# A gated unit with one quantized matmul: the order's cost table repriced, late weight ranges on ScalarE, one rounding step fewer for down_w

## The chip, the cores and the metric

The kernel runs on one core of one Trainium2 chip. The metric is the device time of one execution in microseconds (us); lower is better. Five instruction streams run side by side and wait for each other by semaphores: PE (TensorE), DVE (VectorE), ACT (ScalarE), POOL (GpSimd) and SP (SyncE, which issues nearly all DMAs here). Each stream is carried out strictly in its own order: an instruction that waits holds up everything behind it on its engine.

## The reference

```python
def act_quant(x):      # per token
    scale = 127.0 / clip(max(abs(x), axis=-1, keepdims=True), 1e-05)
    return clip(round(x * scale), -128, 127) / scale
def weight_quant(w):   # one scale for the whole matrix
    scale = 1.0 / clip(mean(abs(w)), 1e-05)
    return clip(round(w * scale), -1, 1) / scale

scale = cond @ norm_w.T + 1.0                       # (4, 512)
h = x * (scale[:, None, :] * rsqrt(mean(x*x, -1) + 1e-6))
u = h @ up_w.T                                      # (4, 1024, 4096)
val, gate = split(u, 2, axis=-1)
h = val * gelu(gate)                                # (4, 1024, 2048)
y = act_quant(h) @ weight_quant(down_w).T + x       # (4, 1024, 512)
```

x is (4, 1024, 512) in float32, cond (4, 128), norm_w (512, 128), up_w (4096, 512), down_w (512, 2048).

## The kernel before

There are four batches of 1024 tokens, and the 2048 hidden features are cut into 16 groups of 128 (index j), each with a gate row block and a value row block of up_w. Weights and activations are split into two float16 parts, so a product takes three float16 matmul terms. The first batch uses the plain product (`plain`, L897 in the profile), half by half of the tokens; while it runs, the weights are loaded, ranged, scaled, turned and their sums built and spilled to `s_dram`. Batches 1 to 3 use seven products of sums in place of eight (`product`, L882, driven by `slot`), and the quantized second matmul of the batch before runs in between (`Pair`, L1153, and `down_mm`, L1102).

Names and steps that the change and the prediction touch:

- `w_range(j)` is `w_largest` (L589: largest magnitude of each row of up_w's two blocks of group j, one DVE reduce) and `w_factor` (power of two of it, its reciprocal); `w_scale` multiplies the rows by it. Only a power of two is needed, so that the rows fit float16.
- down_w comes in eight parts, `d_load(n)`. `d_sum(n)` sums magnitudes on ACT (L744), `d_mean` (L753) brings their mean over the partitions by one matmul, `d_round(n)` scales, clips and rounds on DVE (L759, L760), `d_put(n)` writes the -1, 0, 1 as 8-bit floats on ACT (L769).
- The condition: `scT` holds the row scale of each batch with the features along the partitions. `cond_rows` (L551) writes the columns of batches 1 to 3 to `rows_dram`, three DMAs of 512 single floats each. `cond_load_scale(b)` (L556) reads row b back to every partition as `sc`; `cond_bring(b, sc)` (L560) multiplies it on DVE. The tokens of the next batch are then scaled with it (`Tokens.scale`).
- In `plain_half(j, h)` the gate product goes to bank A or B and through Gelu on ACT, the value product goes to bank E, and a DVE step (L925) multiplies them into H. It is this DVE step that frees the E bank; there are two E banks, taken in turn.

Nothing runs in the order of the source. `Plan` records every instruction as a `Step` with a cost from `price()` (alone, beside a busy neighbour, and for a DMA the time that it holds the queue). `order()` makes 40 rounds: `needed` gives each step the latest time at which it may start, `place` puts the steps one after another, most urgent first, into the first free stretch of their engine, and `replay` runs the resulting order in the model, six times with random misses. The best order is emitted, engine by engine. So a change of a price moves instructions on all five engines. In the model a DMA lands 1.2 us (ISSUE) plus its queue time plus 1.5 us (LANDING) after its issue; the queue time is its bytes by 290, 150 or, for runs under 64 bytes, 1.5 KB per us.

Of the kernel before, what the change touches and what calls it, by code (L numbers as in the profile page):

```python
# [22 lines left out]
P = 128  # L23
EXPONENT = 0x7F800000
MAGIC = 1.5 * 2.0**23
# [2 lines left out]


W_UP = 2.0**12  # L30
X_UP = 2.0**8


# [78 lines left out]
class Plan:  # L112
# [68 lines left out]
    def order(self):  # L181

        steps = self.steps
        for s in steps:
            s.after, s.cost = [], (s.alone + s.beside) / 2
        for s in steps:
            for d in s.deps:
                steps[d].after.append(s)
        clock = 0.0
        for s in steps:  # L190
            if s.eng == "PE":
                s.start = clock
                clock += s.cost
        best, chance = None, random.Random(1)
        for n in range(ROUNDS):
            self.needed(clock)
            self.place(0.3 * (n % 4))
            order = sorted(steps, key=lambda s: (s.start, s.n))
            clock = self.replay(order)
            late = sum(self.replay(order, chance) for _ in range(MISSES)) / MISSES  # L200
            if best is None or late < best[0]:
                best = late, order
            self.replay(order)
        self.replay(best[1])
        return best[1]
# [5 lines left out]
            for t in s.after:  # L211
                s.late = min(s.late, t.late - lag(s, t) - s.wait - s.cost)

    def place(self, margin):

        steps = self.steps
        used = {e: Line() for e in ("PE", "ACT", "DVE", "POOL", "SP", "DMA")}
        for s in sorted(steps, key=lambda s: (s.late, s.n)):  # L220
            t = max((steps[d].end + lag(steps[d], s) for d in s.deps), default=0.0)
            if s.eng != "PE":
                t += min(margin, max(0.0, s.late - t) * 0.1)
            if s.wait and s.eng == "SP":
                t = used["DMA"].put(t + ISSUE, s.wait) - ISSUE
            s.start = used[s.eng].put(t - s.before, s.before + s.cost) + s.before
            s.end = s.start + (ISSUE + s.wait + LANDING if s.wait else s.cost)

    def replay(self, order, chance=None):

        steps = self.steps
        free = dict.fromkeys(("PE", "ACT", "DVE", "POOL", "SP", "DMA"), 0.0)
        port = {"DVE": 0.0, "POOL": 0.0}
        for s in order:
            e = s.eng
            t = free[e] + s.before
# [26 lines left out]


HEAD = 150
ROUNDS, MISSES, ISSUE, LANDING, RELOAD = 40, 6, 1.2, 1.5, 6.5


class Line:
# [2 lines left out]
    def __init__(self):  # L272
        self.spans = []

    def put(self, t, cost):
# [7 lines left out]
        v.insert(n, (t, t + cost))  # L283
        return t


# [9 lines left out]
def price(eng, method, writes, reads, args, kwargs):  # L296

    out = writes[0]
    n = _free(out)
    if "dma" in method:  # L300
        nbytes = n * out.shape[0] * mybir.dt.size(out.dtype)
        if "transpose" in method:
            return 0.45 + nbytes / 32768 * 0.16, 0.0, nbytes / 32768 * 0.17
        last = min(v.ap[-1][1] * mybir.dt.size(v.dtype) if v.ap[-1][0] == 1 else 4 for v in (out, reads[0]))
        return 0.45, 0.0, nbytes / (290e3 if last >= 1024 else 1.5e3 if last < 64 else 150e3)
    wide = max([n] + [_free(v) for v in reads if len(v.shape) > 1])
    psum = any(str(v.space).endswith("PSUM") for v in reads)
    if eng == "PE":
        f32 = any(v.dtype == F32 for v in reads)
        return (max(n, 64) * (2 if f32 else 1) / 2.4 + 2.5) / 1e3, 0.0, 0.0  # L310
    if eng == "ACT":
        cost = 0.08 + wide * 0.0009 + (0.05 if method != "copy" else 0) + (0.05 if psum else 0)
        return cost, 0.0, 0.0
    if eng == "POOL":
        if method == "partition_all_reduce":
            return (1.8 if wide > 1 else 0.4), 0.0, 0.0
        if method == "tensor_scalar":
            cost = 0.2 + wide * 0.00092
            return cost, cost * 1.2, 0.0
        cost = 0.75 if wide <= 8 else 0.18 + wide * 0.00195  # L320
        return cost, cost * 1.42, 0.0
    if method == "reciprocal":
        return 0.17 + max(0, wide - 8) * 0.0056, 0.0, 0.0
    if wide <= 32:
        return 0.17, 0.0 if psum else 0.44, 0.0
    if psum or method in ("tensor_reduce", "memset"):
        return 0.1 + wide * 0.00108, 0.0, 0.0
    if method == "tensor_scalar":
        cost = 0.1 + wide * 0.00052
        return cost, cost * 2.2, 0.0  # L330
# [3 lines left out]
    cost = 0.1 + wide * 0.00106  # L334
    return cost, cost * (1.35 if method == "scalar_tensor_tensor" else 1.8), 0.0


class Rings:
# [30 lines left out]
def glu_quant_kernel(  # L369
# [11 lines left out]
    PE, ACT, DVE, POOL, SP = book.engines(nc)  # L381
# [12 lines left out]
    cpool = ctx.enter_context(tc.tile_pool(name="const", bufs=1))  # L394
# [3 lines left out]
    psum = Rings(banks, {"A": 512, "B": 512, "E": 512, "po": 512})  # L398
# [4 lines left out]
    one = cpool.tile([P, 1], F32, name="one")  # L403
    DVE.memset(one, 1.0)
    ones = one.to_broadcast([P, P])

    R = cpool.tile([P, 2, NA * 2048], F32, name="R")  # L410
# [38 lines left out]
        "p (c w f) -> p c w f", c=7, w=2  # L449
    )  # L450
    A21 = R[:, 0, 6144 : 6144 + 768].bitcast(F16).rearrange("p (n w f) -> p n w f", n=3, w=2)

    def s_tile(g):

# [108 lines left out]
    sw = cpool.tile([P, NJ, 2], F32, name="sw")  # L563
# [6 lines left out]
    def wn(j):  # L570
        return H[:, W_SLOT[j % 3]]
# [14 lines left out]
    def w_largest(j, t0=0, t1=2):  # L586
        t = slice(t0, t1)
        am = sm.tile([P, 2], F32, name=f"wam_{j}_{t0}", tag="wam")[:, t]
        DVE.tensor_reduce(am, wn(j)[:, t], AX.X, ALU.max, apply_absolute_value=True)  # L589
        return am  # L590

    def w_factor(j, am, t0=0, t1=2):
        t = slice(t0, t1)
        pow2_floor(am)
        DVE.tensor_scalar(sw[:, j, t], am, 2.0**-100, 1.0 / W_UP, ALU.max, ALU.mult)
# [130 lines left out]
    wsc = cpool.tile([P, 1], F32, name="wsc")  # L726
# [4 lines left out]
    def d_part(n):  # L731
        return R[:, 1, n * HF : (n + 1) * HF]
# [23 lines left out]

    def d_round(n):
        dn = d_part(n)
        DVE.tensor_scalar(dn, dn, wsc, 1.0, ALU.mult, ALU.min)  # L759
        DVE.tensor_scalar(dn, dn, -1.0, MAGIC, ALU.max, ALU.add)  # L760

    tn = []

    def d_put(n):
        _, u, y = d_at(n)
        if y == 0:
            tn.append(wpool.tile([P, HF], BF16, name=f"tn_{n}", tag="v"))
        t8 = tn[-1].bitcast(F8).rearrange("p (f y) -> p f y", y=2)
        ACT.activation(t8[:, :, y], d_part(n), AF.Copy, bias=-MAGIC, saturate=False)  # L769
        if y:  # L770
            SP.dma_start_transpose(wd[:, n // 4, u], tn[-1])

# [505 lines left out]
    am = w_largest(0, 1, 2)  # L1278
# [317 lines left out]
    for b in range(1, B):  # L1596
        dve, act = Filler(), Filler()
        gains(b)
        am = am_tile(b - 1)
# [42 lines left out]
        for j in range(NJ):  # L1642
# [7 lines left out]
            more = D_SUM_US * len(late_sums) + 0.7 * (j + 1 == min(DOWN) and b + 1 < B)  # L1650
# [77 lines left out]
    am = am_tile(b)  # L1728
# [160 lines left out]
```

## Time and profile before

| what | value |
|---|---|
| runs of the kernel before | 742.14, 742.27 and 743.57 us; median 742.27 |
| the profiled execution | 737.92 us, its span 736.1 us |
| granted TensorE clock in it | 0.998 of full speed |
| PE busy | 723.8 us (98% of the span) |
| DVE, ACT, POOL busy | 606.6 (82%), 392.1 (53%), 215.5 us (29%) |
| DMA queue of SP | 114.76 MB, 60.7% of the 16 engines' span |

The profiled execution is 4.35 us quicker than the median of the runs; its span leaves out 1.8 us of its own time. PE is the engine that is nearly always busy, so the time hangs on the few places where PE waits, and on what stands before its first and behind its last matmul.

### The profile page before, as it was taken

What the parts mean: (1) busy time and instruction counts of PE and PEld (TensorE: products, weight loads), DVE (VectorE), ACT (ScalarE), POOL (GpSimd) and SP (SyncE); (2) the same over time, 40 slices, a digit from 0 to 9 for tenths busy, and PEclk for the clock granted to TensorE, in tenths of its full rate; (3) what the DMA queues carried; (4) which work ended last, traced back from release to release, by engine and by line L of the source; (5) the groups of instructions that cost most, each with busy time, mean ns of one, the idle gap of its engine ahead of it and who ended that gap; (6) DMA issues with size and microseconds to landing.
All of it is one profiled execution on the core that took longest, in us unless ns stands there. A gap on an engine that the chain in (4) does not pass through costs nothing.

```text
span 736.1 us, 10201 instructions
## 1 busy us (share of the span) xinstructions
PE 723.8 (98%) x3684; PEld 363.2 (49%) x3684; DVE 606.6 (82%) x833; ACT 392.1 (53%) x635; POOL 215.5 (29%) x213
## 2 busy tenths in 40 slices
PE   6999999999999999999999999999999999999998
PEld 3554444444444445655444445656444444444754
DVE  5976899999888767989878988798768888865997
ACT  4876646676245775535344577743333666333373
POOL 1465887789214000714002300750001000000000
PEclk9999999999999999999999999999999999999999
DMA  8788678999954444695943445697753444443414
GB/s 267 244 175 206 192 203 210 233 250 236 229 162 101 100 102 137 159 206 154 233 135 101 108 101 140 159 208 155 183 141 106 97 100 108 104 101 97 144 38 164
DMA packets 179567, 115.74 MB, mean 157 GB/s; under 512 B 141750, under 2 KB 147767, under 8 KB 179516
## 3 DMA queue, kind: packets, MB, share of 16 engines
q1 hardware_dynamic: 179226, 114.76, 60.7%
q10 hardware_dynamic: 290, 0.33, 0.3%
q8 instruction: 29, 0.48, 0.3%
q14 instruction: 22, 0.18, 0.1%
HBM read 58.93 MB, written 23.09 MB: 111 GB/s over the span
## 4 chain that ended last, share of the span: by engine, by line
PE 88%; DMA 5%; DVE 3%; ACT 3%; issue 1%; POOL 1%; SPq 0%; POOLq 0%; DVEq 0%
PE A L882 33%; PE E L882 17%; PE B L882 8%; PE po L1153 8%; PE E L897 8%; PE B L897 4%; PE A L897 4%; DMA rows_dram<-scT 2%; PE po L1102 2%; PE E L1102 1%; PE A L1102 1%; DMA s_dram<-R 1%; DMA H<-in_x_dram 1%; DMA am<-in_x_dram 1%; ACT R L1218 1%
## 5 line engine op out<-in xcount | busy, mean ns | idle before, releaser
L882 PEld LDWEIGHTS <-SXY 128*128 128x128 f16 x2016 | 197.2, 98 | 229.8 <-issue 2.1
L882 PE MATMUL A<-R,SXY 128*128 128x512 f16 x1152 | 270.5, 379 | 0.3 <-ACT t L960 0.3
L882 PE MATMUL E<-R,SXY 128*128 128x512 f16 x576 | 142.9, 379 | 0.0
L1032 POOL PARTITION_ALL_REDUCE am<-R x8 | 17.3, 2158 | 249.1 <-DVE R L1018 249.1
L1074 DVE TENSOR_TENSOR H<-H,am 128x1024 f32<-128x1024 f32 x64 | 78.7, 1260 | 0.1
L897 PEld LDWEIGHTS <-SXY 128*128 128x128 f16 x462 | 45.1, 98 | 53.5
L882 PE MATMUL B<-R,SXY 128*128 128x512 f16 x288 | 70.8, 379 | 0.0
L1016 DVE TENSOR_REDUCE gm<-H 128x512 f32<-128x1024 f32 x56 | 68.9, 1230 | 0.7
L980 DVE SCALAR_TENSOR_TENSOR H<-A,sg,t 128x512 f32<-128x512 f32 x48 | 35.9, 748 | 36.0 <-PE A L882 35.7
L968 ACT COPY B<-A 128x512 f32<-128x512 f32 x48 | 27.4, 570 | 60.1 <-PE A L882 56.7
L1153 PE MATMUL po<-wd,R 128*128 128x256 fp8e4 (+1 forms) x448 | 59.0, 275 | 0.0
L993 ACT ACTIVATE t<-t,sg 128x512 f32<-128x512 f32 x48 | 34.7, 722 | 39.2 <-DVE t L990 39.1
L1153 PEld LDWEIGHTS <-R 128*128 128x128 bf16 (+1 forms) x480 | 47.0, 98 | 15.9
L960 ACT COPY t<-A 128x512 f32<-128x512 f32 x48 | 28.1, 586 | 48.9 <-PE A L882 48.8
L990 DVE TENSOR_TENSOR t<-E,t 128x512 f32<-128x512 f32 x48 | 33.0, 688 | 24.4 <-PE E L882 24.0
L977 ACT ACTIVATE t<-B,sg 128x512 f32<-128x512 f32 x48 | 33.0, 687 | 34.5 <-PE B L882 34.0
L786 POOL TENSOR_SCALAR ssq<-ssq 128x2 f32<-128x2 f32 x12 | 5.5, 456 | 155.4 <-ACT H L816 114.1
L897 PE MATMUL E<-R,SXY 128*128 128x512 f16 x210 | 49.6, 379 | 0.0
L996 DVE TENSOR_TENSOR v<-A,v 128x512 f32<-128x512 f32 x48 | 33.1, 689 | 19.7 <-PE A L882 18.0
L972 ACT COPY v<-E 128x512 f32<-128x512 f32 x48 | 28.1, 586 | 34.0 <-PE E L882 31.6
L1018 DVE TENSOR_TENSOR R<-R,gm 128x512 f32<-128x512 f32 x56 | 44.4, 792 | 0.8
L897 PEld LDWEIGHTS <-R 128*128 128x128 f16 x282 | 27.5, 98 | 33.6 <-issue 1.3
(232 smaller groups left out, 1082.0 us busy)
## 6 DMA issues: line engine op xcount, KB each, us to landing
SXY<-s_dram SPq DMA_DIRECT2D x66, 256.0 KB, 2.7
SXY<-s_dram SPq DMA_DIRECT2D x18, 384.0 KB, 3.6
H<-in_L_cond_up_w_dram SPq DMA_DIRECT2D x13, 512.0 KB, 4.9
s_dram<-SXY SPq DMA_DIRECT2D x14, 384.0 KB, 4.9
xr<-in_x_dram SPq DMA_DIRECT2D x19, 256.0 KB, 3.3
out_dram<-xr SPq DMA_DIRECT2D x19, 256.0 KB, 3.6
H<-in_x_dram SPq DMA_DIRECT2D x8, 512.0 KB, 5.5
R<-in_L_cond_down_w_dram SPq DMA_DIRECT2D x8, 512.0 KB, 6.5
```

The costliest lines, as they stand in the source:

```text
L882: PE.matmul(o, s[:, w, k, :], tv[:, :, c, l, k, :], start=start and n == 0, stop=stop and n == len(TERMS) - 1, skip_group_check=True,)
L897: PE.matmul(ps, a[k // 2][:, w, k % 2, :], XP[:, l, k, h * TOK : (h + 1) * TOK], start=n == 0, stop=n == len(terms) - 1,)
L977: ACT.activation(cur["t1"], pb, AF.Gelu, scale=gain(g, 1))
L980: DVE.scalar_tensor_tensor(h_half(g - 1, 0), prev["A"], gain(g - 1, 0), prev["t1"], ALU.mult, ALU.mult)
L990: DVE.tensor_tensor(prev["t2"], prev["E"], prev["t2"], ALU.add)
L993: ACT.activation(prev["t2"], prev["t2"], AF.Gelu, scale=gain(g - 1, 1))
L996: DVE.tensor_tensor(cur["v"], cur["A"], cur["v"], ALU.add)
L1016: DVE.tensor_reduce(gm[0], v, AX.X, ALU.max, apply_absolute_value=True)
L1018: return [largest, lambda: DVE.tensor_tensor(m, m, gm[0], ALU.max)]
L1074: DVE.tensor_tensor(v, v, r.to_broadcast([P, 2, TOK]), ALU.mult)
L1102: PE.matmul(po.rearrange("p (y c o) -> p y c o", c=2, o=P), q[:, a, h, j], wd8[:, :, j // n, j % n, :, y0:y1].rearrange("p c o y -> p y c o"),
L1153: PE.matmul(po, w[:, j], m, start=start and j == 0, stop=stop and j == n - 1, skip_group_check=True,)
```

## The change

Four edits, of which the first moves instructions all over the program:

1. The model of the planner. DMAs issued by other queues than SP's are placed and replayed like SP's. `place` takes a second number (`guard`, a stretch kept free ahead of an urgent step), with four settings of both in turn. Random misses are drawn otherwise. Prices of ACT, DVE and POOL steps are changed.
2. For groups 6 and up, `w_largest` is two ACT passes with Abs and a running sum over the row, in place of one DVE reduce; the sum stands in for the largest value, and W_UP for it is twice as large.
3. `d_round` is one DVE step (scale, then add a large constant, which rounds) and no longer clips; `d_put` takes Sign of the value less that constant.
4. A small constant tile is filled at the start (`nmagic`).

```diff
+BY_SUM = 6
+W_UP_SUM = 2.0**13
...
-            self.place(0.3 * (n % 4))
+            self.place(*MARGINS[n % len(MARGINS)])
...
-    def place(self, margin):
+    def place(self, margin, guard):
...
-            if s.wait and s.eng == "SP":
+            if s.wait > 0.1:
                 t = used["DMA"].put(t + ISSUE, s.wait) - ISSUE
-            s.start = used[s.eng].put(t - s.before, s.before + s.cost) + s.before
+            near = 0.0 if s.eng == "PE" or s.late - t > 1.0 else guard
+            s.start = used[s.eng].put(t - s.before, s.before + s.cost, near) + s.before
...
-                cost *= 1.0 if e == "PE" else 0.95 + 0.14 * chance.random()
+                cost *= 1.0 if e == "PE" else 0.96 + 0.12 * chance.random()
+                if s.beside > s.alone:
+                    cost += 0.6 * (s.beside - s.alone) * chance.random()
...
-            if s.wait and e != "SP":
+            if 0.0 < s.wait <= 0.1:
                 s.end = t + ISSUE + s.wait + LANDING
...
+MARGINS = ((0.3, 0.0), (0.3, 0.15), (0.3, 0.3), (0.25, 0.1))
...
-        cost = 0.08 + wide * 0.0009 + (0.05 if method != "copy" else 0) + (0.05 if psum else 0)
+        cost = 0.12 + wide * 0.0008 + (0.05 if psum else 0)
+        if wide == 512 and method != "copy":
+            cost = 0.62 if psum else 0.7
...
     def w_largest(j, t0=0, t1=2):
...
+        if j >= BY_SUM:
+            for n in range(t0, t1):
+                ACT.activation(w_junk, wn(j)[:, n], AF.Abs, accum_out=am[:, n : n + 1])
+            return am
         DVE.tensor_reduce(am, wn(j)[:, t], AX.X, ALU.max, apply_absolute_value=True)
...
     def d_round(n):
         dn = d_part(n)
-        DVE.tensor_scalar(dn, dn, wsc, 1.0, ALU.mult, ALU.min)
-        DVE.tensor_scalar(dn, dn, -1.0, MAGIC, ALU.max, ALU.add)
+        DVE.tensor_scalar(dn, dn, wsc, MAGIC, ALU.mult, ALU.add)
...
-        ACT.activation(t8[:, :, y], d_part(n), AF.Copy, bias=-MAGIC, saturate=False)
+        ACT.activation(t8[:, :, y], d_part(n), AF.Sign, bias=nmagic, saturate=False)
```

What the new prices do to the order is shown at four places. Lines of the changed kernel are 16 to 21 higher than those of the kernel before: its L567, L572, L576, L917, L945, L774 and L1213 are L551, L556, L560, L897, L925, L753 and L1193 there.

The first place is SP's queue in the first 70 us, in the kernel before. `rows_dram<-scT` is `cond_rows`, `sc<-rows_dram` is `cond_load_scale(1)`, `H<-in_L_cond_up_w_dram` a load of up_w, `xn` and `am` loads of tokens of batch 1:

```order
L693 DMA s_dram<-SXY 128x3584
L740 DMA R<-in_L_cond_down_w_dram 128x1024 x2
L808 DMA xn_109<-in_x_dram 128x2x512
L551 DMA rows_dram<-scT 128x4x1 x2
L693 DMA s_dram<-SXY 128x3584
L581 DMA H<-in_L_cond_up_w_dram 128x2x512
L556 DMA sc_112<-rows_dram 128x512
L808 DMA am_114<-in_x_dram 128x2x512
L581 DMA H<-in_L_cond_up_w_dram 128x2x512
L551 DMA rows_dram<-scT 128x4x1
L693 DMA s_dram<-R 128x3584
```

The same place of SP's queue in the changed kernel:

```order
L714 DMA s_dram<-SXY 128x3584
L761 DMA R<-in_L_cond_down_w_dram 128x1024 x2
L714 DMA s_dram<-SXY 128x3584
L597 DMA H<-in_L_cond_up_w_dram 128x2x512
L828 DMA xn_110<-in_x_dram 128x2x512
L597 DMA H<-in_L_cond_up_w_dram 128x2x512
L567 DMA rows_dram<-scT 128x4x1
L828 DMA am_115<-in_x_dram 128x2x512
L572 DMA sc_113<-rows_dram 128x512
L714 DMA s_dram<-R 128x3584
L567 DMA rows_dram<-scT 128x4x1 x2
L714 DMA s_dram<-SXY 128x3584
```

The first row of the condition went from ahead of two loads of up_w to behind them, with the read of it two places after it; the other two rows follow the read. The second of the two loads of up_w ahead of it waits until PE has turned the weights that lie in its place. On PE, these four transposes (L625 before, L646 now) stood behind the fourth matmul of a gate product into bank B; now they stand in the gate product before it, into bank A, behind the four matmuls that follow the transposes of the group's other block.

The second place is DVE at the same time. Here is the kernel before, from the last range of a weight group to the multiplication of the next half (`gm` is a maximum over H for the token ranges):

```order
L598 RECIPROCAL iv_101<-sw 128x2
L604 TENSOR_SCALAR sg_77<-sw,dx 128x2 x2
L925 TENSOR_SCALAR H<-E_98,sg_77,t_1_104 128x512
L560 TENSOR_SCALAR sc_112<-sc_112,ux 128x512
L1016 TENSOR_REDUCE gm_106<-H 128x512
L660 TENSOR_TENSOR R<-po_97,R 128x256
L1018 TENSOR_TENSOR R<-R,gm_106 128x512
L658 TENSOR_TENSOR R<-po_96,R 128x2x256
```

And DVE in the changed kernel:

```order
L619 RECIPROCAL iv_102<-sw 128x2
L625 TENSOR_SCALAR sg_78<-sw,dx 128x2 x2
L576 TENSOR_SCALAR sc_113<-sc_113,ux 128x512
L1036 TENSOR_REDUCE gm_107<-H 128x512
L945 TENSOR_SCALAR H<-E_99,sg_78,t_1_105 128x512
L775 TENSOR_SCALAR wmean<-po_96 128x1
L776 RECIPROCAL wsc<-wmean 128x1
L780 TENSOR_SCALAR R<-R,wsc 128x1024
```

The step that empties the first of the two E banks stood ahead of `cond_bring`; now it stands behind it and behind a reduce.

The third place is PE right there. In the kernel before (E_98 and E_99 are the two E banks, the `po<-ident,H` rows transposes of weights):

```order
L897 LDWEIGHTS R
L897 MATMUL E_99<-R 128x512
L897 LDWEIGHTS R
L897 MATMUL E_99<-R 128x512
L625 MATMUL po_96<-ident,H 128x128 x4
L897 LDWEIGHTS SXY
L897 MATMUL B_87<-R,SXY 128x512
```

In the changed kernel (E_99 is here the first E bank, E_100 the second):

```order
L917 LDWEIGHTS R
L917 MATMUL E_100<-R 128x512
L774 MATMUL po_96<-wpart_112,one 128x1
L917 LDWEIGHTS R
L917 MATMUL E_99<-R 128x512
L917 LDWEIGHTS R
L917 MATMUL E_99<-R 128x512
L917 LDWEIGHTS R
L917 MATMUL E_99<-R 128x512
```

Where the transposes and a gate product followed, there now follow the mean's matmul and four matmuls into the first E bank, taken from later in the stream.

The fourth place is DVE in batch 2, near 490 us, where the second matmul's third pair ends. L865 casts the tokens of the next batch, L1193 takes a bank of the second matmul out. Before:

```order
L1138 TENSOR_TENSOR R<-R 128x1024
L999 TENSOR_SCALAR H<-v_117,sg_77,t_1_124 128x512
L865 TENSOR_TENSOR H<-H 128x4x256
L1193 TENSOR_SCALAR xr_125<-po_95,dq_127,xr_125 128x256
L1193 TENSOR_SCALAR xr_126<-po_95,dq_127,xr_126 128x256
```

In the changed kernel, where L1157, L1158 and L1019 are L1137, L1138 and L999 of the kernel before:

```order
L1157 TENSOR_TENSOR R<-H,R 128x1024
L1158 TENSOR_TENSOR R<-R 128x1024
L1019 TENSOR_SCALAR H<-v_118,sg_78,t_1_125 128x512
L1213 TENSOR_SCALAR xr_126<-po_96,dq_128,xr_126 128x256
L1213 TENSOR_SCALAR xr_127<-po_96,dq_128,xr_127 128x256
```

The cast of the tokens no longer stands between the multiplication and the two steps that empty the bank; it was moved up.

More of the change, by code (lines that the diff above doesn't have):

```diff
@@ L273, in __init__, with put @@
         self.spans = []
-    def put(self, t, cost):
+    def put(self, t, cost, guard=0.0):
         v = self.spans
@@ L282, in put @@
             n += 1
-        v.insert(n, (t, t + cost))
+        free = v[n - 1][1] if n else 0.0
+        v.insert(n, (max(free, t - guard), t + cost))
         return t
@@ L320, in price @@
         cost = 0.75 if wide <= 8 else 0.18 + wide * 0.00195
-        return cost, cost * 1.42, 0.0
+        return cost, cost * (1.2 if wide > 256 else 1.42), 0.0
     if method == "reciprocal":
@@ L326, in price @@
     if psum or method in ("tensor_reduce", "memset"):
-        return 0.1 + wide * 0.00108, 0.0, 0.0
+        return 0.1 + wide * (0.00116 if wide == 512 else 0.00105), 0.0, 0.0
     if method == "tensor_scalar":
-        cost = 0.1 + wide * 0.00052
-        return cost, cost * 2.2, 0.0
+        cost = 0.08 + wide * 0.00051
+        return cost, cost * 1.85, 0.0
     if method == "tensor_tensor" and all(v.dtype in (BF16, F16) for v in reads):
@@ L333, in price @@
         return cost, cost * 1.6, 0.0
-    cost = 0.1 + wide * 0.00106
-    return cost, cost * (1.35 if method == "scalar_tensor_tensor" else 1.8), 0.0
+    cost = 0.1 + wide * 0.00101
+    more = 1.45 if wide > 512 or method == "scalar_tensor_tensor" else 1.8
+    return cost, cost * more, 0.0
 class Rings:
@@ L405, in glu_quant_kernel @@
     ones = one.to_broadcast([P, P])
+    nmagic = cpool.tile([P, 1], F32, name="nmagic")
+    DVE.memset(nmagic, -MAGIC)
     R = cpool.tile([P, 2, NA * 2048], F32, name="R")
@@ L451, in glu_quant_kernel @@
     A21 = R[:, 0, 6144 : 6144 + 768].bitcast(F16).rearrange("p (n w f) -> p n w f", n=3, w=2)
+    w_junk = R[:, 0, 5888:6144].bitcast(BF16)
     def s_tile(g):
@@ L594, in w_factor @@
         pow2_floor(am)
-        DVE.tensor_scalar(sw[:, j, t], am, 2.0**-100, 1.0 / W_UP, ALU.max, ALU.mult)
+        up = W_UP_SUM if j >= BY_SUM else W_UP
+        DVE.tensor_scalar(sw[:, j, t], am, 2.0**-100, 1.0 / up, ALU.max, ALU.mult)
         if j not in iv:
```

## The prediction

> **What bounds the kernel now.** I read the page first, then the windows, then who PE waited for, then the chain of work in order of time.
>
> ```profile
> span 736.1 us, 10201 instructions
> ...
> PE 723.8 (98%) x3684; PEld 363.2 (49%) x3684; DVE 606.6 (82%) x833; ACT 392.1 (53%) x635; POOL 215.5 (29%) x213
> ```
>
> PE is idle for 12.3 us of 736.1 (736.1 - 723.8). The windows say where; the second column of a row is its length, the third PE's busy time in it:
>
> ```profile
> 0.00:20.00 20.00, 13.70 (x55) 7.26 (x55) 11.10 (x56) 9.13 (x20) 2.56 (x8) 0.91 0.75 246
> ...
> 60.00:80.00 20.00, 18.95 (x93) 9.13 (x91) 16.05 (x31) 15.72 (x28) 13.84 (x16) 1.00 0.59 153
> ...
> 220.00:260.00 40.00, 39.71 (x186) 18.12 (x185) 31.38 (x37) 25.21 (x35) 8.82 (x8) 1.00 0.40 95
> ...
> 460.00:500.00 40.00, 39.02 (x252) 24.50 (x251) 35.05 (x44) 22.99 (x47) 25.16 (x24) 1.00 0.75 169
> ...
> 720.00:736.10 16.10, 12.61 (x75) 7.06 (x72) 11.82 (x18) 5.17 (x5) 0.00 (x0) 1.00 0.45 164
> ```
>
> 6.3 us are lost before the first weights and tokens are there, 3.5 us behind the last matmul, and between them only 1.05, 0.29 and 0.98 us (another 0.16 stands in 20 to 40 us). So a better order can win some 2.5 us at the most, and a worse one can lose more: PE has no slack to give a wait back. The waits of PE name the middle two:
>
> ```profile
> PE E L897 <- DVE H L925: 1.0, 1, 1.0
> PE po L1153 <- DVE xr L1193: 1.0, 1, 1.0
> ```
>
> The chain of work between 40 and 80 us shows what stands behind the first:
>
> ```profile
> 41.38 12.25 DMA rows_dram<-scT
> ...
> 54.08 6.37 DMA am<-in_x_dram
> ...
> 64.65 7.88 DMA s_dram<-R
> ...
> 79.19 1.02 PE E L897 x4
> ```
>
> The reader is to see that the small scatter of the condition is the longest piece of this chain: 12.25 us from its issue to its landing, for 2 KB. It cost nothing itself, because nobody needed it soon.
>
> **The change, part by part.** The edits of the work itself come first, by groups of instructions (after the bar: busy time in all, mean ns of one):
>
> ```profile
> L589 DVE TENSOR_REDUCE wam<-H 128x2 f32<-128x1024 f32 (+1 forms) x17 | 19.5, 1147 | 4.2 <-DMA H<-in_L_cond_up_w_dram 4.2
> ...
> L760 DVE TENSOR_SCALAR R<-R 128x1024 f32<-128x1024 f32 x8 | 8.8, 1123 | 0.0
> ...
> L769 ACT ACTIVATE v<-R 128x1024 fp8e4<-128x1024 f32 x8 | 8.4, 1052 | 1.1 <-DVE R L760 0.9
> ...
> L816 ACT ACTIVATE xt<-xn 128x512 f32<-128x512 f32 x12 | 7.5, 626 | 1.6 <-DMA xn<-in_x_dram 1.5 <-DVE nx L865 0.2
> ...
> L816 ACT ACTIVATION_READ_ACCUMULATOR xt<-xn 128x1 f32 x12 | 2.3, 189 | 0.0
> ```
>
> Ten groups (6 to 15) lose a reduce of 1.15 us, so DVE is rid of 11.5 us, and of 8 x 1.12 = 9.0 us with the second rounding step. ACT takes on 20 passes; no such pass with Abs on 512 elements is in the trace, the nearest is the sum of squares, 0.63 us and 0.19 us for reading the sum out: 20 x 0.82 = 16 us. `d_put` with Sign in place of a copy I take at the same 1.05 us. All of it lies between 60 and 190 us, where every window but the quoted one shows PE fully busy, and ACT has room (15.7 of 20 us in that one). I cost this edit at zero for the end; without that cover, 16 us of ACT against 20 us of DVE in one stretch would shift a wait by tenths. The fill of one constant at the start I take at zero too (under 0.1 us on DVE).
>
> The new order is what counts. **The gain** is at 495 us:
>
> ```profile
> 492.76 1.74 DVE L865 TENSOR_TENSOR H<-H 128x1024 f16<-128x1024 f32 x1
> ...
> 493.98 0.38 PE L882 MATMUL A<-R,SXY 128*128 128x512 f16 x1
> ...
> 494.42 0.86 DVE L1193 SCALAR_TENSOR_TENSOR xr<-po,dq,xr 128x256 f32<-128x256 f32 x2
> ...
> 495.34 0.27 PE L1153 MATMUL po<-wd,H 128*128 128x256 fp8e4 x1 [0.98 <-DVE xr L1193]
> ```
>
> PE waits for the pair of steps at 494.42, which stood behind a cast of 1.74 us. The order of the changed kernel has no cast between; the pair comes up to 1.74 us earlier, and the wait goes: 495.34 - 493.98 less one matmul of 0.2 is 1.15 us. I take 1.1 us; next late there are steps that were on time before.
>
> **The loss** is near 67 us. These are the rows of the kernel before:
>
> ```profile
> 41.38 0.97 SPq L551 DMA_DIRECT2D rows_dram<-scT  x2
> ...
> 50.58 1.67 PE L897 MATMUL A<-R 128*128 128x512 f16 x7
> ...
> 53.70 0.33 SPq L556 DMA_DIRECT2D sc<-rows_dram  x1
> ...
> 55.54 0.60 PE L625 MATMUL po<-ident,H 128*128 128x128 f32 x4
> ...
> 56.17 0.37 SPq L581 DMA_DIRECT2D H<-in_L_cond_up_w_dram  x1
> 56.60 0.94 SPq L551 DMA_DIRECT2D rows_dram<-scT  x1
> ...
> 66.75 0.60 PE L625 MATMUL po<-ident,H 128*128 128x128 f32 x4
> 66.87 0.74 DVE L925 SCALAR_TENSOR_TENSOR H<-E,sg,t 128x512 f32<-128x512 f32 x1
> ...
> 67.53 0.47 DVE L560 TENSOR_SCALAR sc<-sc,ux 128x512 f32<-128x512 f32 x1
> ...
> 67.92 1.23 DVE L1016 TENSOR_REDUCE gm<-H 128x512 f32<-128x1024 f32 x1
> ```
>
> Step by step. (a) The first row of the condition was issued at 41.38. Now it follows a load of up_w which waits for the four transposes of 55.54; these come after four of the seven matmuls at 50.58 (each 1.67 less 0.17 of the last one's run-out, by 7: 0.21 us), so at 51.4, and end at 52.0. The load goes at 52.0, the row at 52.4 (0.4 behind, as 56.60 behind 56.17): 11 us later than before. (b) How long it takes and the read of it after it, by the DMA view (us to landing last):
>
> ```profile
> sc<-rows_dram SPq DMA_DIRECT2D x3, 256.0 KB, 4.3
> ...
> rows_dram<-scT SPq DMA_DIRECT2D x3, 2.0 KB, 12.1
> ...
> dq<-am_dram SPq DMA_DIRECT2D x2, 2.0 KB, 2.4
> ```
>
> SP issues the read when the row has landed (53.70 follows 41.38 by 12.3 us), and tokens, spills and two more rows of the condition wait behind it on SP. With the rows' 12.1 and 4.3 us, `sc` is there at 68.8. Two rows of 512 single floats went together at 41.38, behind two parts of down_w and a load of tokens; now it is one, behind one load. That can take off what lay ahead in the queue, so I take 11.0 and 4.2: `sc` at 67.6. (c) On DVE, `cond_bring` (0.47) waits for that, the reduce (1.23) and the multiplication that frees the E bank (0.74) stand behind it, with three hand-overs of 0.05: 2.6 us, so the bank is free at 70.2. (d) PE reaches the four matmuls into this bank where the kernel before stood at 66.75, plus one small matmul for the mean: 66.8. It waits 70.2 - 66.8 = 3.4 us. Before, the multiplication was done at 67.6 without any DMA and the bank was used much later.
>
> From below, the nearest small transfer took 2.4 us; with it nothing waits at all, since the read then lands at 59.1, and the wait is zero from a landing of `sc` at 64.2 downwards. From above, 12.25 for the row and the 6.37 us that the chain shows behind the first read give 71.0 and a wait of 6.8 us. I take 3.4, near the rows of the very same transfer.
>
> [...]
>
> What else moves? The other two rows are issued together behind the read, with a spill of 896 KB behind them. In the chain the spill at 64.65 took 7.88 us with the third row 8 us ahead of it. That chain led to the 1.05 us of wait at 79.19. In the new order the spill from R goes ahead of those rows, the one from SXY behind; I leave the 1.05 as it is, with 1 us on either side. Head and tail keep their order but for single steps, zero with 0.3 on either side.
>
> Sum: 3.4 - 1.1 = +2.3 us. The profiled execution would go from 737.92 to 740.2, its span from 736.1 to 738.4. The runs' median was 742.27; the same difference gives 744.6.
>
> **The rivals.**
>
> *The row lands in time (faster).* Place: `cond_bring` on DVE. The point is `sc` at 64.2, that is 11.8 us for row and read together. For it: the 2.4 us of the other 2 KB transfer, a queue with less ahead, one row in place of two. Against: 12.25 us in the chain, 12.1 in the DMA view. [...] The rival gives -1.1, or -2.2 if the wait at 79.19 goes too, since then the spill no longer stands behind the rows: 740.1 to 741.2.
>
> *Wait and gain cancel.* Row and read take 12 to 14.4 us, the wait is 0.2 to 2.6 us: 741.4 to 743.8.
>
> *The wait is long.* Row and read take 12.25 and 6.37 us as in the chain, or the spill behind the two later rows holds up the loads of up_w behind it as the 7.88 us did: wait 5 to 6.8, with 1 us more at 79: +3.9 to +6.7, 746.2 to 749.
>
> *The edits don't take work off DVE.* The prices move the steps anyway and PE has no DVE wait left of that kind; it changes none of these sums.
>
> **How the numbers follow.** A measurement here tells about 0.2%, 1.5 us. The forecast (wait 2.6 to 5 us, 743.8 to 746.2) has 0.50, the long wait 0.11, cancelling 0.19, in time 0.20, of which 0.13 with the wait at 79.19 gone too (-2.2) and 0.07 without (-1.1). Slower by over 0.2% is the forecast and the long wait, 0.61; within 0.2% cancelling and the smaller part of in time, 0.26; faster 0.13. The range 740.6 to 748.0 takes in the forecast, the cancelling, most of in time and the lower part of the long wait; it leaves out at most 2 in 10.
>
> **What would show it.** In the profile of the changed kernel: `cond_bring` on DVE, near 68 us, waiting for the DMA of `sc`; PE waiting 2 to 5 us for the multiplication into H, in the window 60 to 80, whose PE time falls to 14 to 17 us; the row's issue near 52 and the read's near 63; no wait at L1213 near 495. Wrong would be: `sc` landed before 64, PE waiting somewhere else by more than 1.5 us, or the window 460 to 500 still short of 1 us.

## The result and the profile after

| | before | changed |
|---|---|---|
| runs, us | 737.47 to 743.57, median 741.45 (12 runs) | 743.22 to 748.06, median 746.31 (12 runs) |
| profiled execution, us | 737.92, span 736.1 | 745.51, span 743.7 |
| ratio | | 1.0068, 95% interval 1.0047 to 1.0089 |

The changed kernel is slower: 0.0068 of 741.45 us is 5.0 us (3.5 to 6.6 by the interval). The forecast was +2.3 us. The time lies inside the predicted range, near its upper end, but just above the forecast's own band (743.8 to 746.2) and at the lower edge of the rival "the wait is long". The page of the changed kernel, with the busy time of the engines:

```profile
span 743.7 us, 10243 instructions
PE 725.1 (97%) x3684; PEld 362.7 (49%) x3684; DVE 595.4 (80%) x816; ACT 405.5 (55%) x675; POOL 213.0 (29%) x213
```

DVE has lost 11.2 us of work and ACT has gained 13.4, in the direction that the edits meant. The groups taken off DVE held 20.9 us before (12.1 of ranges, 8.8 of rounding), against 20.5 forecast; not all of it shows, because other steps of DVE took longer in sum. PE was idle for 18.6 us in place of 12.3. Its windows, with the granted clock behind the engines' columns:

```profile
0.00:20.00 20.00, 14.61 (x65) 6.89 (x66) 13.16 (x61) 11.20 (x23) 3.14 (x8) 1.00 0.69 233
...
60.00:80.00 20.00, 14.51 (x62) 7.13 (x61) 7.57 (x13) 7.61 (x15) 6.29 (x9) 0.83 0.82 100
80.00:100.00 20.00, 17.32 (x81) 7.78 (x80) 19.93 (x19) 15.86 (x26) 18.11 (x16) 1.00 0.81 241
...
460.00:500.00 40.00, 40.00 (x248) 24.16 (x247) 32.43 (x42) 19.69 (x39) 20.20 (x23) 1.00 0.75 172
```

460 to 500 us is full now: the wait of 0.98 us there is gone. 60 to 80 us lost 5.5 us of PE's time and 80 to 100 us 2.7. PE there, in order of time:

```profile
64.48 0.28 PE L774 MATMUL po<-wpart,one 128*128 128x1 f32 x2
69.79 1.87 PE L917 MATMUL E<-R 128*128 128x512 f16 x4 [5.03 <-DVE H L945]
71.45 1.70 PE L646 MATMUL po<-ident,H 128*128 128x128 f32 x7
73.62 0.48 PE L646 MATMUL po<-ident,H 128*128 128x128 f32 x1 [0.46 <-ACT R L672]
73.88 3.42 PE L917 MATMUL B<-R,SXY 128*128 128x512 f16 x12
...
86.90 1.02 PE L917 MATMUL E<-R 128*128 128x512 f16 x4 [2.69 <-DVE H L945]
```

There are two waits, 5.03 and 2.69 us. Behind the first PE runs at half speed: four matmuls take 1.87 us, those at 86.90 take 1.02, and the granted clock is 0.83 in 60 to 80 us and 1.00 in 80 to 100. What the queue of SP and the waiting engines did:

```profile
50.27 0.46 SPq L567 DMA_DIRECT2D rows_dram<-scT  x1
...
61.80 0.34 SPq L572 DMA_DIRECT2D sc<-rows_dram  x1
62.24 0.38 SPq L714 DMA_DIRECT2D s_dram<-R  x1
62.67 1.52 SPq L567 DMA_DIRECT2D rows_dram<-scT  x2
64.30 1.68 SPq L714 DMA_DIRECT2D s_dram<-SXY  x1
```

```profile
67.46 0.49 DVE L576 TENSOR_SCALAR sc<-sc,ux 128x512 f32<-128x512 f32 x1 [6.26 <-DMA sc<-rows_dram]
...
69.00 0.74 DVE L945 SCALAR_TENSOR_TENSOR H<-E,sg,t 128x512 f32<-128x512 f32 x1
```

```profile
76.51 0.59 ACT L670 CAST R<-po 128x512 f16<-128x512 f32 x1 [2.94 <-DMA s_dram<-R]
```

```profile
77.12 0.69 DVE L679 TENSOR_TENSOR R<-po,R 128x512 f16<-128x512 f32 x1 [2.57 <-ACT R L670]
```

```profile
64.30 17.26 DMA s_dram<-SXY
```

The reader is to see two chains. One is the forecast's: row, read, `cond_bring`, multiplication, E bank. The other was given only a tolerance: the spill from R, issued at 62.24, is waited for by ACT until 76.51, and DVE waits for ACT until 77.12. From there DVE works without a gap over 0.2 us up to the multiplication of 86.11 to 86.85 that PE's second wait ends with. The spill from SXY takes 17.26 us in the chain of work. Both spills stand beside three rows of the condition.

### The profile page after: what moved, and what is told of

The parts are those of the page before. It is cut to its first block, busy times and chain, and to the rows that moved or that the text cites. A ratio compares the mean times of both kernels' runs of the same rounds, so it can differ in the third digit from the quotient of the medians.

```text
span 743.7 us, 10243 instructions
## 1 busy us (share of the span) xinstructions
PE 725.1 (97%) x3684; PEld 362.7 (49%) x3684; DVE 595.4 (80%) x816; ACT 405.5 (55%) x675; POOL 213.0 (29%) x213
## 4 chain that ended last, share of the span: by engine, by line
PE 91%; DVE 4%; DMA 3%; ACT 1%; issue 1%; SPq 0%; DVEq 0%; ACTq 0%
PE A L902 33%; PE E L902 17%; PE E L917 10%; PE po L1173 8%; PE B L902 8%; PE A L917 6%; PE B L917 5%; DMA s_dram<-SXY 2%; DVE H L1094 2%; DMA H<-in_x_dram 1%; PE A L1122 1%; PE B L1173 0%; PE po L646 0%; DVE am L1063 0%; PE A L960 0%
## 5 line engine op out<-in xcount | busy, mean ns | idle before, releaser
L1052 POOL PARTITION_ALL_REDUCE am<-R x8 | 15.6, 1946 | 285.5 <-DVE R L1038 285.5
L917 PEld LDWEIGHTS <-SXY 128*128 128x128 f16 x462 | 45.4, 98 | 54.5 <-issue 0.8
L917 PE MATMUL E<-R,SXY 128*128 128x512 f16 x210 | 49.7, 379 | 0.0
L917 PE MATMUL E<-R 128*128 128x512 f16 x162 | 39.9, 385 | 7.7 <-DVE H L945 7.7
L917 PEld LDWEIGHTS <-R 128*128 128x128 f16 x282 | 27.7, 99 | 40.2 <-issue 8.6
L1102 ACT ACTIVATE H<-H 128x1024 f32<-128x1024 f32 x38 | 40.0, 1056 | 8.6 <-DVE H L1094 8.6
L1038 DVE TENSOR_TENSOR R<-R,gm 128x512 f32<-128x512 f32 x56 | 42.9, 765 | 0.9
```

The source lines that it names most:

```text
L917: PE.matmul(ps, a[k // 2][:, w, k % 2, :], XP[:, l, k, h * TOK : (h + 1) * TOK], start=n == 0, stop=n == len(terms) - 1,)
L1038: return [largest, lambda: DVE.tensor_tensor(m, m, gm[0], ALU.max)]
L1102: ACT.activation(v, v, AF.Copy, bias=MAGIC)
```

## The experiments

Two theories were put against each other. A: PE waits because the multiplication stands behind `cond_bring`. B: what counts is that spills and loads beside the single floats land late, whatever stands in front on DVE. The moves were written into the finished order, so that nothing else changed; each pair is (step, the step it goes ahead of):

```diff
-        return best[1]
+        return moved(best[1])
...
+def moved(order):
+    for n, m in MOVES:
+        s = next(s for s in order if s.n == n)
+        order.remove(s)
+        order.insert(next(i for i, t in enumerate(order) if t.n == m), s)
+    return order
```

**bring_late.** Step 758 is `cond_bring`, 657 the mean's step on DVE.

```diff
+MOVES = ((758, 657),)
```

> The changed kernel, with one step moved on DVE: cond_bring goes behind the multiplication that frees the E bank (and ahead of the mean's step). Nothing else moves. Theory A (the prediction's chain: PE waits because the multiplication stands behind cond_bring): the wait of 5.0 us at 64.5 us goes, and with it the half-speed matmuls behind it (2.3 us); the wait of 2.7 us at 84 us stays: 7 us less than the changed kernel, 739 us. Theory B (the spill from R, which lands only at 76.5 us, holds up ACT and DVE whatever stands in front): PE's wait only moves, from 64.5 to the stretch 72 to 86 us, and grows there to 8 to 10 us: within 1 us of the changed kernel, 745.5 to 747 us.

Measured: median 742.94 us, ratio 1.0063 (1.0037 to 1.0089), the loss as before, though two of the eleven runs are quick (735.48 and 736.18 us). PE, ACT and the chain of work:

```profile
78.00 1.02 PE L928 MATMUL E<-R 128*128 128x512 f16 x4 [2.99 <-DVE H L956]
82.56 1.86 PE L928 MATMUL E<-R 128*128 128x512 f16 x4 [3.54 <-DVE H L956]
```

```profile
72.17 0.58 ACT L681 CAST R<-po 128x512 f16<-128x512 f32 x1 [6.18 <-DMA s_dram<-R]
```

```profile
60.31 11.84 DMA s_dram<-R
```

The wait near 64 us is gone and comes back later, as 2.99 and 3.54 us, less than the 8 to 10 us that B gave. Theory A told truly what PE waited for, and it was not what the time hung on; the time goes with B.

**rows_early and others_early.** Steps 523 to 525 are the three rows, 678 the read of the first, 359 a spill from SXY near 43 us, 759 the second load of tokens.

```diff
+MOVES = ((523, 359), (524, 359), (525, 359), (678, 759))
```

> The changed kernel, with SP's queue changed: the three rows of the condition go behind the two parts of down_w (near 41 us), and the read of the first row goes ahead of the second load of batch 1's tokens. Theories A and B alike: cond_bring finds its row there at 61 us, the spills from R and SXY have no row near them, both waits of PE (5.0 with 2.3 of half speed, and 2.7 us) go: 9 to 10 us less than the changed kernel, 736 to 738 us, quicker than the kernel before. Theory C (the cause is elsewhere in the new order, for example the multiplications into the E banks are late by themselves): over 743 us.

```diff
+MOVES = ((524, 359), (525, 359))
```

> The changed kernel, with the two later rows of the condition issued near 43 us, so that no row stands behind the spill from R; the first row and its read stay where they are. If the spill (14.3 us from issue to landing) is held up by the two rows issued right behind it: it lands in 5 to 8 us, the wait of 2.7 us at 84 us goes, the first wait stays at 4 to 5 us: 2.7 us less, 743.6 us. If it is held up by the first row and its read, which stand ahead of it: it still takes 12 us or more, and the time stays within 1 us, 745.5 to 747 us.

Measured: 743.77 us, ratio 1.0092 (1.0072 to 1.0111), and 744.70 us, 1.0104 (1.0081 to 1.0126). Neither time fell as expected; that of rows_early is the one that its theory C gave, and rows_turned, below, speaks against C. The chain and PE's longest wait, rows_early first, then others_early:

```profile
44.31 13.27 DMA s_dram<-SXY
```

```profile
71.35 1.87 PE L928 MATMUL E<-R 128*128 128x512 f16 x4 [4.34 <-DVE H L956]
```

```profile
54.14 15.44 DMA rows_dram<-scT
```

```profile
75.78 1.87 PE L928 MATMUL E<-R 128*128 128x512 f16 x4 [5.82 <-DVE H L956]
```

Going early doesn't help: the spill issued behind three rows together is held up (13.27 us), and a row behind two others, a spill and loads takes 15.44 us itself. The harm moves with the rows. One half of others_early's question is answered all the same: with the read right ahead of it, but no row behind it, the spill from R, issued at 70.03, had landed within 9.4 us, since ACT's cast behind it, at 79.44, did not wait for a DMA; in the changed kernel it took 14.3.

**kept_busy.** 22 matmuls into the free B bank stand in the wait.

```diff
+        for _ in range(22):
+            nc.tensor.matmul(pz, XP[:, 0, 0, :P], XP[:, 0, 0, :TOK], start=True, stop=True)
```

> The changed kernel, with 22 matmuls more on PE behind the mean's matmul (into the B bank, which is free there, result not used): they fill 4.75 us of the wait of 5.0 us. Theory of the clock: the idle stretch is what halves the rate of the matmuls behind it, so with PE kept busy their pitch goes from 0.43 back to 0.22 us, 2.3 us less there; by A the time falls by 2.3 us to 744 us, by B the wait at 84 us grows by what was won and the time stays within 1 us. If the half speed has another cause, the pitch stays at 0.43 us.

Measured: 740.53 us, ratio 1.0051 (1.0025 to 1.0077). PE:

```profile
65.36 4.91 PE L1890 MATMUL B<-R 128*128 128x512 f16 x22
70.11 1.03 PE L922 MATMUL E<-R 128*128 128x512 f16 x4
70.97 0.93 PE L651 MATMUL po<-ident,H 128*128 128x128 f32 x7
...
72.53 2.75 PE L922 MATMUL B<-R,SXY 128*128 128x512 f16 x12
...
83.51 1.02 PE L922 MATMUL E<-R 128*128 128x512 f16 x4 [1.33 <-DVE H L950]
```

The same three groups of matmuls took 1.87, 1.70 and 3.42 us in the changed kernel, and the granted clock of 60 to 80 us is 1.00 here in place of 0.83: the half speed came from the idle stretch and cost 0.84 + 0.77 + 0.67 = 2.3 us there. The later wait was 1.33 us, neither the 2.69 of A nor longer as B had it. The interval overlaps that of the changed kernel (1.0047 to 1.0089), so the profile shows the half speed and its cause, and the runs alone don't show the saving.

**rows_turned and before_turned.** The three writes become one of 12 runs of 512 bytes, at the place of the first. The second kernel is the kernel before with the same.

```diff
+        nc.vector.tensor_copy(cols, scT[:, :, 1:].rearrange("p k b -> p b k"))
+        nc.tensor.transpose(pt, cols.rearrange("p b k -> p (b k)"), ident)
+        nc.scalar.copy(rows_sb, pt)
+        nc.sync.dma_start(out=rows_dram[1:].rearrange("b (k p) -> (b k) p", p=P), in_=rows_sb)
```

> The changed kernel in its own order, with the three writes of the condition's rows (512 single floats each) replaced, at the place of the first, by one write of 12 runs of 512 bytes: a DVE copy, one PE transpose into a bank that is free there, an ACT copy, one DMA. Theory A (what counts is when the first row is readable): the row is there 3 us after its issue in place of 11.5, the read is done by 58 us, the first wait (5.0 us and 2.3 us of half speed) goes. Theory B (what counts is that the spills and loads land late beside the single floats): the spill from R lands in 4 to 5 us in place of 14.3, and the second wait goes too. Both together: no wait of PE over 0.5 us between 60 and 90 us, 10 us less than the changed kernel, ratio to the kernel before 0.993 to 0.996. If the waits come from the new order itself, the ratio stays at 1.005 or more.

> The kernel before in its own order with the same replacement of the three writes. Its only wait in that stretch is the 1.05 us at 79 us. Theory B: the spill from R at 64.65 us lands in 4 to 5 us in place of 7.9, and the 1.05 us go: ratio 0.998 to 0.999. Theory A: nothing waits for the rows there, the ratio is 1.000.

Measured: rows_turned 736.70 us, ratio 0.9992 (0.9979 to 1.0004); before_turned 736.79 us, 0.9996 (0.9983 to 1.0010). The DMA view (us to landing last) of the changed kernel, then SP, the same DMA row and PE of rows_turned:

```profile
s_dram<-SXY SPq DMA_DIRECT2D x4, 896.0 KB, 17.7
```

```profile
53.82 0.38 SPq L1894 DMA_DIRECT2D rows_dram<-rows_sb  x1
...
55.77 0.34 SPq L579 DMA_DIRECT2D sc<-rows_dram  x1
```

```profile
s_dram<-SXY SPq DMA_DIRECT2D x4, 896.0 KB, 3.7
```

```profile
79.03 1.02 PE L924 MATMUL E<-R 128*128 128x512 f16 x4 [0.90 <-DVE H L952]
...
201.95 0.38 PE L909 MATMUL A<-R,SXY 128*128 128x512 f16 x1 [1.24 <-DVE v L1023]
```

The read follows the write by 1.95 us in place of 11.5, the large spills from SXY land in 3.7 us in place of 17.7 (of the four, the view can tell the landing of one in the changed kernel, the one issued at 64.30, and of two here), and the whole loss is gone, with DVE in the changed kernel's order. So the scatter of single floats, at its new place in SP's queue, carries the loss. It isn't the 0.993 to 0.996 expected: 0.90 us stay at 79, and 1.24 us at 202, where the kernel before has none, stand in place of the gain at 495, and behind 700 us PE is idle for 4.41 us where it was 3.49 in the kernel before. The ratio of before_turned does not decide between its two theories, 1.000 and 0.998 to 0.999; it shows that at their old place the rows cost little or nothing.

**before_two_behind.** In the kernel before, steps 522 and 523 are the later rows, 580 the load of up_w behind the spill from R.

```diff
+MOVES = ((522, 580), (523, 580))
```

> The kernel before, with the two later rows of the condition moved behind the spill from R (64.7 us), as the changed kernel has them; the first row and its read stay early, and DVE's order stays, with the multiplication ahead of cond_bring. Theory A (PE waits for the row by way of cond_bring): the read is early, nothing waits: ratio 1.000. Theory B (spills and loads beside the single floats land late): the spill takes 12 to 15 us in place of 7.9, the wait of 1.05 us at 79 us grows to 5 to 9 us with half speed behind it: ratio 1.006 to 1.014.

Measured: 741.70 us, ratio 1.0071 (1.0049 to 1.0092). The chain, ACT and PE:

```profile
67.16 11.37 DMA H<-in_L_cond_up_w_dram
```

```profile
67.91 0.61 ACT L660 CAST R<-po 128x512 f16<-128x512 f32 x1
```

```profile
81.27 1.86 PE L908 MATMUL E<-R 128*128 128x512 f16 x4 [4.43 <-DVE H L936]
```

With DVE's old order and an early first row, two moved rows alone make a loss of this size. The load behind them took 11.37 us. The spill from R ahead of the rows, issued at 63.29, was not held up, other than expected: ACT's cast that has to wait for it, the step that waited until 76.51 in the changed kernel, started at 67.91, 4.6 us after the issue, without waiting.

**prices_only and edits_only.** Each has half of the change, with an order that its planner makes of it: prices_only has the first edit alone, edits_only the other three. Parts of both are shown, against the changed kernel.

```diff
-        if j >= BY_SUM:
-            for n in range(t0, t1):
-                ACT.activation(w_junk, wn(j)[:, n], AF.Abs, accum_out=am[:, n : n + 1])
-            return am
...
-        DVE.tensor_scalar(dn, dn, wsc, MAGIC, ALU.mult, ALU.add)
+        DVE.tensor_scalar(dn, dn, wsc, 1.0, ALU.mult, ALU.min)
+        DVE.tensor_scalar(dn, dn, -1.0, MAGIC, ALU.max, ALU.add)
```

> The kernel before with the first edit alone (the planner's placing and prices), the work as it was: the ranges on DVE, two steps of rounding. SP's queue in the first 80 us comes out as in the changed kernel (first row behind two loads of up_w, two rows behind the spill from R). Both theories: the same waits of about 5 and 3 us near 65 and 84 us, ratio 1.005 to 1.010. If the edits of the work carry the loss (ACT's passes in the stretch), the ratio is near 1.000.

```diff
-            self.place(*MARGINS[n % len(MARGINS)])
+            self.place(0.3 * (n % 4))
...
-MARGINS = ((0.3, 0.0), (0.3, 0.15), (0.3, 0.3), (0.25, 0.1))
```

> The kernel before with edits 2 to 4 alone (ranges of groups 6 and up on ACT, one rounding step, the constant), under the old planner, which makes an order of its own from them: two rows of the condition behind the loads of up_w and tokens with the read one load later, the third row between the spills from R and SXY, cond_bring again ahead of the multiplication that frees the E bank. Theory of the prediction for the edits themselves: they cost nothing, ratio 1.000. Theory B (what counts is where the rows of single floats fall in SP's queue): this order is bad too, with waits of PE between 60 and 90 us: ratio 1.003 to 1.010.

Measured: prices_only 745.78 us, ratio 1.0113 (1.0093 to 1.0132); edits_only 747.84 us, 1.0136 (1.0115 to 1.0158); both lose more than was expected. PE of prices_only, then PE and the chain of edits_only:

```profile
67.56 1.02 PE L906 MATMUL E<-R 128*128 128x512 f16 x4 [1.65 <-DVE H L934]
...
79.89 1.02 PE L906 MATMUL E<-R 128*128 128x512 f16 x4 [1.12 <-DVE H L934]
83.83 1.87 PE L906 MATMUL E<-R 128*128 128x512 f16 x4 [2.91 <-DVE H L934]
```

```profile
79.66 1.86 PE L908 MATMUL E<-R 128*128 128x512 f16 x4 [3.47 <-DVE H L936]
84.22 1.87 PE L908 MATMUL E<-R 128*128 128x512 f16 x4 [2.69 <-DVE H L936]
```

```profile
46.69 11.92 DMA rows_dram<-scT
59.11 16.66 DMA s_dram<-R
```

The planner's edit alone brings the loss. The edits of the work alone bring it too, and their trace shows the order that the old planner makes of them at fault: two rows near 47 us, the third right behind the spill from R, which takes 16.66 us. Either half puts rows beside what is soon needed.

**after_again, cast_later, both_mended.** The changed kernel once more; the kernel before with the cast at 492.8 us (step 4131) behind the two bank steps; and that with the turned rows.

```diff
+MOVES = ((4131, 3486),)
```

> The changed kernel itself once more, on the chip of this call. Measured before: ratio 1.0068. If the size of the loss depends on how the rows and spills meet in each execution, waits of PE between 60 and 90 us of 5 to 10 us again but otherwise divided; the ratio between 1.005 and 1.012.

> The kernel before with one step moved on DVE: the cast of tokens at 492.8 us (1.74 us) goes behind the two steps that empty the bank of the second matmul at 494.4 us. It is the gain of the prediction by itself: the wait of 0.98 us at 495 us goes and PE ends 1.1 us earlier, ratio 0.9985. If something else is late right behind it, the ratio is 1.000.

> The kernel before with both repairs: the rows of the condition turned on PE and written in runs of 512 bytes (the wait of 1.05 us at 79 us goes), and the cast moved (1.1 us at 495 us). PE then has no wait over 0.5 us behind 20 us: 2 us less, ratio 0.997; below 1 beyond the interval, if head and tail do not hide it.

Measured: after_again 744.56 us, ratio 1.0087 (1.0067 to 1.0107); cast_later 736.25 us, 0.9988 (0.9976 to 1.0001); both_mended 736.66 us, 0.9990 (0.9977 to 1.0003). PE of after_again, and one window each of cast_later and both_mended:

```profile
71.68 1.02 PE L917 MATMUL E<-R 128*128 128x512 f16 x4 [3.36 <-DVE H L945]
72.54 1.39 PE L646 MATMUL po<-ident,H 128*128 128x128 f32 x7
...
74.66 3.55 PE L917 MATMUL B<-R,SXY 128*128 128x512 f16 x12
...
88.11 1.02 PE L917 MATMUL E<-R 128*128 128x512 f16 x4 [2.99 <-DVE H L945]
```

```profile
100.00:700.00 600.00, 600.00 (x3076) 300.72 (x3075) 499.17 (x628) 305.96 (x492) 153.16 (x146) 1.00 0.60 151
```

```profile
100.00:700.00 600.00, 599.71 (x3078) 301.03 (x3077) 498.85 (x630) 306.66 (x492) 154.18 (x146) 1.00 0.60 151
```

The two places wait again in the changed kernel, 3.36 and 2.99 us, and half speed comes again behind the first, this time within the transposes (1.39 and 3.55 us against 0.93 and 2.75 in kept_busy). The cast's move takes the wait at 495 us away, and 0.0012 of 736.88 is 0.9 us against 1.1 forecast; the interval still holds 1. both_mended has no wait of PE left over 0.3 us in that window, but its runs (733.90 to 738.13 us) aren't quicker than cast_later's: it is not shown to beat the kernel before. One reason stands in the trace of cast_later: with its rows still written as single floats it has no wait at 79 us either (PE is idle for 0.14 us in 20 to 100 us), so in that execution the turned rows had nothing left to win. How often the kernel before has that wait is open.

## Why the prediction was right or wrong

**The gain** (-1.1 us): right. The window 460 to 500 is full, and alone, in cast_later, it measured 0.9 us, with an interval that just takes in no gain at all.

**Loss (a) and (b)**, when the row can be read: right, by two errors that cancel. The head of the two profiled executions differs; two rows of PE of the kernel before and one of the changed kernel:

```profile
12.42 0.87 PE L1242 MATMUL po<-ident,H 128*128 128x128 f32 x3 [3.63 <-DVE wam L467]
...
17.27 0.39 PE L940 MATMUL B<-R,SXY 128*128 128x512 f16 x1 [0.68 <-ACT SXY L649]
```

```profile
15.31 0.39 PE L960 MATMUL B<-R,SXY 128*128 128x512 f16 x1 [0.68 <-ACT SXY L670]
```

The row went out at 50.27, not 52.4, since PE was 2 us earlier from its head on (15.31 against 17.27); row and read took 11.5 + 5.7 us (50.27 to 61.80, 61.80 to 67.46), not 15.2. `sc` came at 67.46 against 67.6. That the two cancel is luck: the head differs from execution to execution, and in after_again the matmul of 15.31 stands at 17.37 again.

**(c) and (d)**: the step ends at 69.74 against 70.2, but PE arrived at 64.76, not 66.8. The wait was 5.03 us, and 3.36 in after_again, against 3.4. What the forecast took it to be was wrong, though. bring_late removes this wait and the time stays: behind it stood the spill, which stops PE 10 to 18 us later if nothing has stopped it sooner (bring_late's waits of 2.99 and 3.54 us).

**The term that failed** is "I leave the 1.05 as it is, with 1 us on either side". The spill from R was noted as going ahead of the two rows; it stands 0.4 us ahead of them and right behind the first row's read, and it landed with 14.3 us from its issue (76.51 - 62.24). The later wait was 2.69 and 2.99 us, not 1.05. The rival "the wait is long" told of a spill that is late beside the rows, with a tenth of the chance. The prediction had also named its own sign of being wrong, a wait of PE over 1.5 us somewhere else, and the wait of 2.69 us is one.

**A cost left out**: half speed behind the long wait, 2.3 us. The profile before showed it: its head has the wait of 3.63 us above, and a granted clock of 0.91 in 0 to 20 us. Behind 20 us, half speed stood behind waits of 5.03, 4.34 and 3.54 us (changed kernel, rows_early, bring_late: four matmuls in 1.86 or 1.87 us), full speed behind 1.33 and 2.99 (kept_busy, after_again: 1.02 us). The bound is not sharp: behind 3.36 us (after_again) the four matmuls still took 1.02 us and the seven transposes after them 1.39 in place of 0.93, behind 2.91 (prices_only) the four took 1.87 at once. The granted clock agrees: between 60 and 100 us it falls to between 0.76 and 0.91 in one of the two windows of 20 us in the eight profiled executions with a wait of 2.91 us or more there, and is 1.00 in both in the six without.

The clock records of the kernel before and of the changed kernel say more. In the changed kernel the clock fell to half at 68.40 us and came back at 75.23, 6.83 us later; in the kernel before it fell at 12.49, in the head, and came back at 15.90, 3.41 us later, half as much. The next fall, behind the last matmul, came 669.0 and 720.2 us after that, 196.0 and 211.0 times 3.41. In the 3.41 us just before 68.40 PE was idle throughout, in those before 12.49 for 3.34 us. With both traces divided into such stretches, counted from their falls, none at full speed with up to 1.9 us of idle time (1.93 in 737.42 to 740.83 of the changed kernel) was followed by half speed; what lies between 1.93 and 3.34 us these two don't show. That fits a wait that counts by how much of it falls into one such stretch; the changed kernel's 2.69 us, without half speed behind it, fell into two, with 1.26 and 1.43 us.

**The edits at zero**: right in the sense that rows_turned, with all of them, stands at 0.9992. Their own order under the old planner stands at 1.0136, so an edit that moves the planner is not priced by its operations alone.

The sum in the profiled executions: PE's idle time in 20 to 720 us went from 2.5 to 8.2 us (+5.7), half speed +2.3, so +8.0 in place of +2.3. Of the difference the first wait has 1.6 us, the later wait 1.6 and half speed 2.3. Head and tail were put at zero with 0.3 on either side, and that was wrong too: behind 700 us PE was idle for 5.03 us in place of 3.49 (4.82 in after_again), and the head won the 1.9 us that are left to the 7.6 by which the spans differ. The runs differ by 5.0, and in after_again by 6.4 (0.0087 of 736.88): the profiled execution of the kernel before is among its quickest, and the spread of each kernel's runs (6.1 us before, 4.8 after) is wider than the gain. One profiled execution gives the mechanism better than the size. That the time lies in the predicted range is in part luck, since the range was wide enough to take in a loss whose larger part the forecast had not priced.

## What to carry to other kernels

A transfer of 2 KB can be the costliest thing in a queue when it is written as single floats (11.5 us here from its issue to the read behind it): price it by its landing and by what is issued beside it, and look at who needs those neighbours soon. When a wait is traced to a step in front of it, ask what would be late next if that step were gone; here the answer was the same time. A wait of PE of about 3 us or more is to be priced with the half-speed matmuls that can follow it: behind 20 us the waits from 3.36 us up all brought them here, one of 2.91 did, and those of 2.69 and 2.99 that PE met at full speed did not.

## What the runs showed of the hardware that was not expected

- 512 single floats written to memory took 9.9 to 15.4 us to land (kept_busy, others_early), and the spills and loads that were held up beside them 11.4 to 17.3 us (before_two_behind, changed kernel), against 3.7 to 4.5 us for the large spills without them (rows_turned, before_turned). It is not the moving of the data that takes the time: in the changed kernel the packets of the first row, issued at 50.27, were over by 53.8 us, and SP could issue the read only at 61.80. The same data in 12 runs of 512 bytes let the read go 1.95 us after the write. The runs don't tell the size of a run from the number of runs, which fell from 1536 to 12 with it.
- A spill issued 0.4 us ahead of two rows was held up in the changed kernel (14.3 us) and not in before_two_behind (at most 4.6). In the first a read of the row stands right ahead of it. That read alone doesn't do it either: others_early has it, with no row behind the spill, and the spill had landed within 9.4 us. Both together held it up in the changed kernel, in prices_only (11.5 us) and in edits_only (16.7 us). How the two work together is not shown.
- The runs of one kernel lie further apart with the rows in the way (bring_late 735.48 to 745.87 us, the kernel before beside it 735.32 to 739.40). The two quick runs of bring_late have a granted clock of 1.000, the nine others 0.990 to 0.995, so the quick ones were hardly at half speed. Why has no profile and stays open.
